# A four-layer graph network on one core: a filler ahead of the first data, quarter work of layer 2 gathered, folding cut, last projections reordered

## The chip, the cores and the metric

The kernel runs on one core of a Trainium2 chip. The time is the device time of one execution in microseconds; the figure for the kernel before is the median of three runs. A profile of one further execution is used to see where the time goes. Engines are called TensorE (PE, with PEld for its weight loads), VectorE (DVE), ScalarE (ACT), GpSimd (POOL) and SyncE (SP), which issues the DMAs.

## What is computed

The input x is 128 graphs of 64 nodes with 512 features (float32), with one 64 by 64 adjacency matrix `adj`. Four layers follow, each of the form `x = x + f(relu(layernorm(x)))`:

```python
# layer 0: 8 heads of 64, masked softmax attention
q, k, v = h @ Wq + bq, h @ Wk + bk, h @ Wv + bv
x = x + softmax(q k^T / 8 + mask) v
# layer 1: the same, with an output projection:  x = x + (attention) @ Wo + bo
# layer 2: no softmax
rel = adj.T * ((h Wq^T) (h Wk^T)^T)
x = x + (rel / norm(rel, axis=2)) (h Wv^T)
# layer 3: attention without biases, o = (attention) @ w_proj + b_proj
x = x + o + layernorm(o) * gamma + beta
```

All of it is float32.

## The kernel before

**Tiling.** Eight graphs, 512 tokens, make a block. There are `NB` = 16 blocks per layer and N = 64 block steps, walked by one loop, `for n in range(N)` (line 976), layer by layer. A block's tokens lie in four tiles of 128 tokens (`NT`); features in four chunks of 128 (`KC`). The state between layers goes through DRAM.

**Projections.** A 512 by 512 by 512 projection is done by Strassen's scheme (Winograd's form, `projection`, line 535): seven products of 256-sided blocks, each four 128x256 matmuls (eight records in a trace). `sums_x` forms the four sums of the input's blocks, `sums_w` (350) those of the weight's blocks (WT1 to WT4). The products run in the order `ORDER = (1, 6, 5, 2, 7, 3, 4)`; they use three PSUM banks in turn (`ps_mm`, tile "mm"), which VectorE and ScalarE evict. Products 1 and 2 read only the input blocks of tokens 0 to 255.

**Quarter work.** Two graphs share a tile of 128 tokens, so scores, weighted sums and relations of one graph are 64 wide and run on 64-row parts of TensorE, four at a time (`QUARTERS`). They write the two "so" buffers (`ps_so`). `attend` (651) does the scores, softmax and the turn of the weights, and calls `finish0` or `finish13` for the weighted sum. `relate` (870) is layer 2: it multiplies hT by gT (gT holds h times the folded matrix Wq^T Wk), masks (`rel`), squares (`sq`), sums the squares by matmuls with a column of ones, and weighs v. There the quarter matmuls stand in three groups: the relation; the sums with the first half of the weighing; the second half.

**Folding.** While layer 0 runs, `fold` (397) multiplies wq2 and wk2 into a2d, transposes wv2 on TensorE into v2d, and multiplies the bias bv1 of layer 1's v through wo1 into a row b1.

**Start.** The first block of x, then q0's weight blocks are loaded (`load_w`, 336: W11, b12, W22, W21). Layer norm of block 0 writes transposes through `ps_t`, which has one buffer, and ScalarE copies them into hT. VectorE sums q0's and k0's weights.

**End.** The output projection of a block follows in the next step, after that step's v: step 63 runs q, k, v of block 63 and then o of block 62. The last block's own output projection is a plain one, tile by tile, with its layer norm per tile (lines 1045 to 1069).

**Order.** Operations are recorded by `Plan` and put in order by a list scheduler (`Plan.order`, 130) with estimated durations; within an engine a step that reads an "mm" tile is preferred by `RUSH` places. The order of recording comes from generators that are spawned with a delay counted in products (`spawn`, `tick`, 934 to 945). The order on every engine is then fixed in the program. Line 192, through which every operation is issued, is the line that a trace shows for nearly all.

Of the kernel before, what the change touches and what calls it, by code (L numbers as in the profile page):

```python
# [12 lines left out]
F32 = mybir.dt.float32  # L13
U16 = mybir.dt.uint16
AF = mybir.ActivationFunctionType
ALU = mybir.AluOpType
# [27 lines left out]
ORDER = (1, 6, 5, 2, 7, 3, 4)  # L44

# [173 lines left out]
RUSH = 60  # L219
AHEAD = 16  # L220
# [37 lines left out]
def gnn_stack_kernel(  # L258
# [37 lines left out]

    def dma(dst, src):
        plan.sync.dma_start(dst, src)
# [6 lines left out]
    def row_bc(name, src):  # L305
        t = rows.tile([P, D], F32, tag="row", name=name)
        dma(t, src.partition_broadcast(P))
        return t
# [27 lines left out]
    def load_w(name, src):  # L336

        w = wp.tile([P, 7, 2, H2], F32, tag="w", name=name)
        b12 = p2.tile([P, 2, H2], F32, tag="b12", name=f"b12_{name}")

        def part(i, j):
            return src[i * H2 : (i + 1) * H2, j * H2 : (j + 1) * H2].rearrange("(c p) f -> p c f", p=P)

        dma(w[:, W11], part(0, 0))
        dma(b12, part(0, 1))
        dma(w[:, W22], part(1, 1))
        dma(w[:, W21], part(1, 0))
        return w, b12
# [43 lines left out]
    def raw(tag, src, nm):  # L392
        t = p1.tile([P, KC, D], F32, tag=tag, name=nm)
        dma(t, src.rearrange("(c p) f -> p c f", p=P))
        return t

    def fold():

        rq, rk = raw("oT", wq2, "rq"), raw("SO", wk2, "rk")
        yield 8  # L400
        for dc in range(KC):
            pa = ps_t.tile([P, D], F32, tag="t", name=f"pfa_{dc}")
            plan.begin()
            for ec in range(KC):
                pe.matmul(pa, rq[:, ec, ts(dc, P)], rk[:, ec, :], start=(ec == 0), stop=(ec == KC - 1))
            plan.end()
            f = p2.tile([P, D], F32, tag="z", name=f"fa_{dc}")
            act.copy(f, pa)
            yield 1
            dma(a2d[dc * P : (dc + 1) * P, :], f)  # L410
            yield 1
        rv, ro = raw("oT", wv2, "rv"), raw("SO", wo1, "ro")
        yield 8
        for dc in range(KC):
            pt = ps_t.tile([P, D], F32, tag="t", name=f"pft_{dc}")
            plan.begin()
            for ec in range(KC):
                pe.transpose(pt[:, ts(ec, P)], rv[:, ec, ts(dc, P)], ident)
            plan.end()
            f = p2.tile([P, D], F32, tag="z", name=f"ft_{dc}")  # L420
            act.copy(f, pt)
            yield 1
            dma(v2d[dc * P : (dc + 1) * P, :], f)
            yield 1

        bvm = p2.tile([P, KC, P], F32, tag="z", name="bvm")
        dve.tensor_copy(bvm, bvc1.unsqueeze(2).to_broadcast([P, KC, P]))
        pb = ps_t.tile([P, D], F32, tag="t", name="pb")
        plan.begin()
        for ec in range(KC):  # L430
            pe.matmul(pb, bvm[:, ec, :], ro[:, ec, :], start=(ec == 0), stop=(ec == KC - 1))
        plan.end()
        b1 = row_bc("b1", bo1)
        dve.tensor_tensor(b1, pb, b1, ALU.add)
        R["b1"] = b1
# [17 lines left out]
    hTs, Ss = {}, {}  # L453
# [13 lines left out]
    def layer_norm(n):  # L467
# [19 lines left out]
        if n == 0:  # L487
            for t in range(NT):
                z = xins[n][t]
                act.activation(z, z, AF.Relu, bias=nb[:, t : t + 1], scale=rs[:, t : t + 1])  # L490
                pt = ps_t.tile([P, KC, P], F32, tag="t", name=f"pz_{n}_{t}")
                plan.begin()
                for c in range(KC):
                    pe.transpose(pt[:, c, :], z[:, ts(c, P)], ident)
                plan.end()
                act.copy(hT[:, :, ts(t, P)], pt)
# [38 lines left out]
    def projection(prod, w, xop, nm, emit):  # L535
# [13 lines left out]
        for i in ORDER:  # L549
# [23 lines left out]
            if i != ORDER[-1]:  # L573
                yield
# [194 lines left out]
    def finish13(n):  # L769
        def done(aTs, v):  # L770
# [19 lines left out]
            for g, po in enumerate(pos):  # L790
                for b in range(2):
                    act.copy(o5[:, b, 2 * g : 2 * g + 2], po[:, b])
# [77 lines left out]
    def relate(n, hT, gT, v):  # L870

        prt = ps_so.tile([P, 2, D], F32, tag="so", name=f"pr_{n}")
        pr = prt[:, 0, : NT * G].rearrange("p (t i) -> p t i", t=NT)
        plan.begin()
        for p in range(NT):
            for kc in range(KC):
                for b in range(2):
                    at = ts(2 * p + b, G)
                    pe.matmul(
                        pr[half(b), p, :], hT[:, kc, at], gT[:, kc, at], start=(kc == 0), stop=(kc == KC - 1)  # L880
                    )
        plan.end(300)
        yield 1
        rel = p2.tile([P, NT, G], F32, tag="s", name=f"rel_{n}")
        dve.tensor_tensor(rel, pr, adj2.unsqueeze(1).to_broadcast([P, NT, G]), ALU.mult)
        yield 1
        sq = p2.tile([P, NT, G], F32, tag="aT", name=f"sq_{n}")
        act.activation(sq, rel, AF.Square)
        yield 6
        assert ("xo", n) in ready and ("v", n) in ready  # L890

        pqs = prt[:, 1, :NT], prt[:, 0, NT * G : NT * G + NT]
        pos = [ps_so.tile([P, 2, 2, H2], F32, tag="so", name=f"pv_{n}_0")]

        def weigh(g, po):
            for p in range(2):
                for b, y in QUARTERS:
                    j = b ^ y
                    pe.matmul(
                        po[half(y), j, p, :], rel[half(b), 2 * g + p, :],  # L900
                        v[half(b), 2 * g + p, j * H2 : (j + 1) * H2], start=True, stop=True,
                    )

        plan.begin()
        for p in range(NT):
            for b, y in QUARTERS:
                pe.matmul(
                    pqs[b ^ y][half(y), p : p + 1], sq[half(b), p, :], ones[half(b), :], start=True, stop=True
                )
        weigh(0, pos[0])  # L910
        plan.end(300)
        ss = sm.tile([P, 2, NT], F32, tag="ss", name=f"ss_{n}")
        for j in range(2):
            dve.tensor_copy(ss[:, j], pqs[j])
        pos.append(ps_so.tile([P, 2, 2, H2], F32, tag="so", name=f"pv_{n}_1"))
        plan.begin()
        weigh(1, pos[1])
        plan.end()
        rn = sm.tile([P, 2, NT], F32, tag="rn", name=f"rn_{n}")
        gps.tensor_tensor(rn.rearrange("p j t -> p (j t)"), ss.rearrange("p j t -> p (j t)"), mhalf, ALU.pow)  # L920
        yield 1
        for t in range(NT):
            for j in range(2):
                xo = xos[n][:, t, j * H2 : (j + 1) * H2]
                dve.scalar_tensor_tensor(xo, pos[t // 2][:, j, t % 2], rn[:, j, t : t + 1], xo, ALU.mult, ALU.add)
            yield t % 2
        store(n, xos[n])
# [31 lines left out]
    for name, got in zip(("q0", "k0"), first):  # L959
        W[name] = got[0]  # L960
        now(sums_w(*got, dve))
# [13 lines left out]
    pending_out = None  # L975
    for n in range(N):
# [3 lines left out]
        if n == 3 * NB // 16:  # L980
            spawn(fold(), 2)
        if l == 0 and k == 9 * NB // 16:
            want("q1")
        if l == 2 and k == NB // 2:
            R["bp"], R["gam"], R["bet"] = row_bc("bp", bp3), row_bc("gam", gam3), row_bc("bet", bet3)
        if n + 1 < N:
            load_x(n + 1)
            spawn(layer_norm(n + 1), 5 if l != 2 else 2)
        if l != 2:
            qT = p1.tile([P, KC, T], F32, tag="qT", name=f"qT_{n}")  # L990
            q_emit = emit_bias(region_T(qT), (bqc0, bqc1)[l]) if l < 2 else emit_plain(region_T(qT))
            run(projection(prod_T, W[f"q{l}"], xop, f"q_{n}", q_emit))
# [11 lines left out]
            spawn(attend(n, qT, kT, v, done), 3)  # L1004
# [4 lines left out]
        else:  # L1009
# [4 lines left out]
            v = p1.tile([P, NT, D], F32, tag="v", name=f"v_{n}")  # L1014
            spawn(relate(n, hTs[n], gT, v), 2)
            spawn(load_xo(n), 2)
# [4 lines left out]

        if pending_out is not None:
            m = pending_out
            lm = m // NB
            assert ("xo", m) in ready and m in SOs
            sop = lambda m=m: SOs[m]
            if lm == 1:
                run(projection(prod_N, W["o1"], sop, f"o_{m}", emit_out1(m)))
                spawn(tail1(m))
                if m == 2 * NB - 1:  # L1030
                    want("k3")
            else:
                o = p1.tile([P, NT, D], F32, tag="kT", name=f"o_{m}")
                run(projection(prod_N, W["o3"], sop, f"o_{m}", emit_out3(m, o)))
                spawn(tail3(m, o))
        pending_out = n if l in (1, 3) else None
        if l in (1, 3):
            spawn(load_xo(n), 4)
# [7 lines left out]
    o3 = p1.tile([P, NT, D], F32, tag="kT", name="o_last")  # L1046
    mv = sm.tile([P, NT, 2], F32, tag="mv", name="mv_last")
    rs = sm.tile([P, NT], F32, tag="rs", name="rs_last")
    for t in range(NT):
# [15 lines left out]
        gps.tensor_tensor(xo, xo, o, ALU.add)  # L1065
# [39 lines left out]
```

## Time and profile before

| | us |
|---|---|
| median of three runs | 2864.86 (2864.85 to 2867.84) |
| the profiled execution's own time | 2866.66 |
| its span, first to last instruction | 2864.9 |
| busy: PE, PEld | 2839.8, 2459.5 |
| busy: DVE, ACT, POOL | 1990.4, 1281.1, 1833.9 |
| granted TensorE clock, mean | 0.999 |

Busy shares are means over stages with different limits. In the lines of the chain of work that ended last, the columns are start, length and what ran, with the number of records. In lines of the timeline they are start, length, engine, source line, operation, output and inputs by the names of the program's buffers, shapes and count, and in brackets the idle time before and what ended it. A ring's buffers share a name: "mm" and "so" are the PSUM tiles named above, "t" is `ps_t`, "kT" also holds the output of a projection in layer 3, "s" also rel, "aT" also sq, "qT" also gT, "oT" and "SO" also raw weights during folding. The end of a matmul is modelled; the spacing of records is more exact than their length.

### The profile page before, as it was taken

How to read it: one execution, taken by the hardware profiler on the slowest of the kernel's cores; microseconds unless marked ns; L12 is line 12 of the kernel's file. 1: busy time of each engine (PE TensorE's matmuls, PEld its weight loads, DVE VectorE, ACT ScalarE, POOL GpSimd, SP SyncE). 2: the span in 40 equal slices, each digit the busy share in tenths (PEclk: the TensorE clock that was granted, in tenths of full speed). 3: DMA queues.
4: the chain of work that ended last, by engine and by line, in shares of the span. 5: the costliest groups of instructions: out<-in, count | busy, mean ns of one | idle time of the engine just before them, and what ended most of it. 6: DMA issues, size and time to landing. Idle time of an engine off the chain costs nothing.

```text
span 2864.9 us, 62358 instructions
## 1 busy us (share of the span) xinstructions
PE 2839.8 (99%) x26080; PEld 2459.5 (86%) x26080; DVE 1990.4 (69%) x3019; ACT 1281.1 (45%) x1656; POOL 1833.9 (64%) x1349
## 2 busy tenths in 40 slices
PE   8999999999999999999999999999999999999998
PEld 7888888888888888888888888888888888888887
DVE  6767777877757657567566554555588788888787
ACT  4554555454554534534534434344334444444441
POOL 5556566656766657657677343435578688787796
PEclk9999999999999999999999999999999999999999
DMA  5675656566443533534546656565433433533531
GB/s 148 164 170 128 141 132 144 121 131 165 104 119 79 124 95 85 134 78 96 130 115 170 149 139 157 142 142 147 103 85 95 116 83 90 126 85 86 129 71 63
DMA packets 629515, 342.31 MB, mean 119 GB/s; under 512 B 480880, under 2 KB 559984, under 8 KB 629232
## 3 DMA queue, kind: packets, MB, share of 16 engines
q1 hardware_dynamic: 629232, 338.32, 48.9%
q8 instruction: 204, 3.34, 0.5%
q14 instruction: 79, 0.65, 0.1%
HBM read 153.66 MB, written 69.21 MB: 78 GB/s over the span
## 4 chain that ended last, share of the span: by engine, by line
PE 97%; DVE 2%; issue 1%; POOL 1%; DMA 0%; ACT 0%; POOLq 0%; DVEq 0%; ACTq 0%
PE mm L192 87%; PE so L192 9%; PE t L192 1%; DVE z L192 0%; DVE st L192 0%; DVE kT L192 0%; POOL s L192 0%; DVE xo L192 0%; DVE zp L192 0%; POOL S L192 0%; DVE u L192 0%; DVE mv L192 0%; DMA xin<-in_x_dram 0%; DVE sr L192 0%; POOL ve L192 0%
## 5 line engine op out<-in xcount | busy, mean ns | idle before, releaser
L192 PE MATMUL mm<-S,w 128*128 128x256 f32 x3584 | 819.8, 380 | 3.8 <-DVE kT L192 1.3
L192 PEld LDWEIGHTS mm<-S,w 128*128 128x128 f32 x3584 | 676.8, 190 | 104.0 <-issue 8.4
L192 PE MATMUL mm<-hT,w 128*128 128x256 f32 x2688 | 632.7, 381 | 0.2 <-ACT s L192 0.2
L192 DVE TENSOR_TENSOR u<-mm,s 128x512 f32<-128x512 f32 x414 | 285.3, 689 | 476.3 <-PE mm L192 336.6
L192 PEld LDWEIGHTS mm<-hT,w 128*128 128x128 f32 x2688 | 509.6, 190 | 75.3 <-issue 5.4
L192 PE MATMUL mm<-w,S 128*128 128x256 f32 x2048 | 472.6, 381 | 0.7 <-DVE kT L192 0.6
L192 PEld LDWEIGHTS mm<-w,S 128*128 128x128 f32 x2048 | 385.3, 190 | 55.8 <-DVE kT L192 1.5
L192 PE MATMUL mm<-w,hT 128*128 128x256 f32 x1536 | 366.3, 381 | 0.0
L192 ACT COPY hT<-hp 128x1024 uint16<-128x1024 uint16 x252 | 334.1, 1359 | 71.4 <-DMA hp<-zp 55.5
L192 ACT COPY s<-mm 128x512 f32<-128x512 f32 x207 | 121.0, 585 | 532.2 <-PE mm L192 438.0
L192 POOL TENSOR_TENSOR s<-s,mx 128x1024 f32<-128x1024 f32 x96 | 184.2, 1920 | 251.7 <-DVE mx L192 251.7
L192 PEld LDWEIGHTS mm<-w,hT 128*128 128x128 f32 x1536 | 289.1, 190 | 41.0 <-issue 0.5
L192 ACT COPY aT<-hp 128x1024 uint16<-128x1024 uint16 x188 | 253.3, 1352 | 155.4 <-DMA hp<-zp 155.2
L192 POOL TENSOR_TENSOR xo<-xo,row 128x512 f32<-128x512 f32 x192 | 283.1, 1494 | 4.3 <-DMA xo<-x 3.3
L192 DVE COPY zp<-s 128x1024 uint16<-128x1024 uint16 x188 | 276.5, 1494 | 2.8 <-POOL s L192 2.0
L192 DVE COPY zp<-xin 128x1024 uint16<-128x1024 uint16 x252 | 241.9, 973 | 39.0 <-ACT xin L192 33.1
L192 ACT ACTIVATE xin<-xin,nb,rs 128x512 f32<-128x512 f32 x256 | 196.0, 812 | 104.9 <-DVE nb L192 104.9
L192 PE MATMUL mm<-w,SO 128*128 128x256 f32 x992 | 224.3, 379 | 0.0
L192 POOL TENSOR_TENSOR S<-hT 128x512 f32<-128x512 f32 x126 | 162.1, 1287 | 94.6 <-ACT hT L192 94.6
L192 PEld LDWEIGHTS mm<-w,SO 128*128 128x128 f32 x992 | 188.4, 190 | 26.0 <-issue 0.4
L192 POOL TENSOR_TENSOR s<-s,sr 128x1024 f32<-128x1024 f32 x96 | 187.4, 1963 | 27.4 <-DVE sr L192 26.5
L192 POOL TENSOR_TENSOR v<-u,z 128x512 f32<-128x512 f32 x64 | 82.2, 1285 | 183.6 <-DVE u L192 169.5
(100 smaller groups left out, 3600.3 us busy)
## 6 DMA issues: line engine op xcount, KB each, us to landing
xin<-x SPq DMA_DIRECT2D x192, 256.0 KB, 3.9
xo<-x SPq DMA_DIRECT2D x64, 512.0 KB, 5.6
xin<-in_x_dram SPq DMA_DIRECT2D x64, 256.0 KB, 3.2
x<-xo SPq DMA_DIRECT2D x64, 256.0 KB, 2.5
x<-xo SPq DMA_DIRECT2D x128, 128.0 KB, 2.5
x<-xo SPq DMA_DIRECT2D x32, 512.0 KB, 3.0
out_dram<-xo SPq DMA_DIRECT2D x30, 512.0 KB, 2.8
xo<-in_x_dram SPq DMA_DIRECT2D x32, 256.0 KB, 3.7
```

Of the source, the lines that this page charges most:

```text
L192: getattr(getattr(self.nc, eng), op)(*a, **k)
```

## The change

- 22 transposes of the identity into a "t" tile are put ahead of everything on TensorE.
- The first projection (q of block 0) has the order (1, 2, 5, 6, 3, 7, 4). Every weight loads W21 second. q0's weight sums go to GpSimd. The first transposes use the three "mm" banks; ScalarE copies the first, VectorE the other three.
- `fold` no longer multiplies bv1 through wo1: layer 1's weighted sum gets the bias at eviction, on VectorE in place of ScalarE's copy. wv2 is transposed by a u16 copy, a transposing DMA and a copy back (`turn`).
- `relate` takes up the block before: one group holds that block's norm sums and weighing and this block's relation. Each norm sum is made once instead of twice; two copies cross the halves. A last call in layer 3 finishes layer 2's last block. The relation uses the "t" tile.
- In the last step the output projection of block 62 comes before v of block 63, and the last block's attention starts without delay. The last tiles' residual addition goes from GpSimd to VectorE. Two output tiles use a weight buffer.

```diff
+ORDER0 = (1, 2, 5, 6, 3, 7, 4)
+WARM = 22
+    pw = ps_t.tile([P, KC, P], F32, tag="t", name="pw")
+    for i in range(WARM):
+        pe.transpose(pw[:, i % KC, :], ident, ident)
         dma(w[:, W11], part(0, 0))
+        dma(w[:, W21], part(1, 0))
         dma(b12, part(0, 1))
         dma(w[:, W22], part(1, 1))
-        dma(w[:, W21], part(1, 0))
...
-        for dc in range(KC):
-            pt = ps_t.tile([P, D], F32, tag="t", name=f"pft_{dc}")
-            for ec in range(KC):
-                pe.transpose(pt[:, ts(ec, P)], rv[:, ec, ts(dc, P)], ident)
-            f = p2.tile([P, D], F32, tag="z", name=f"ft_{dc}")
-            act.copy(f, pt)
+        for ec in range(KC):
+            f = p2.tile([P, KC, P], F32, tag="z", name=f"ft_{ec}")
+            turn(f, rv[:, ec, :], f"v2_{ec}")
             yield 1
-            dma(v2d[dc * P : (dc + 1) * P, :], f)
+            dma(v2d.rearrange("(c p) e -> p c e", p=P)[:, :, ts(ec, P)], f)
-        for ec in range(KC):
-            pe.matmul(pb, bvm[:, ec, :], ro[:, ec, :], start=(ec == 0), stop=(ec == KC - 1))
-        dve.tensor_tensor(b1, pb, b1, ALU.add)
...
-                pt = ps_t.tile([P, KC, P], F32, tag="t", name=f"pz_{n}_{t}")
+                pt = ps_mm.tile([P, KC, P], F32, tag="mm", name=f"pz_{n}_{t}")
-                act.copy(hT[:, :, ts(t, P)], pt)
+                (dve.tensor_copy if t else act.copy)(hT[:, :, ts(t, P)], pt)
...
-                    act.copy(o5[:, b, 2 * g : 2 * g + 2], po[:, b])
+                    at = o5[:, b, 2 * g : 2 * g + 2]
+                    if n // NB == 1:
+                        bias = bvc1.unsqueeze(1).unsqueeze(3).to_broadcast([P, 2, KC, G])
+                        dve.tensor_tensor(at, po[:, b], bias, ALU.add)
+                    else:
+                        act.copy(at, po[:, b])
...
+    held = []
+    def relate(n, hT=None, gT=None):
+        prt = ps_t.tile([P, D], F32, tag="t", name=f"pr_{n}")
+        old = held.pop() if held else None
+        plan.begin()
+        if old:
+            m, rel, sq, v = old
+            for p in range(NT):
+                for b in range(2):
+                    pe.matmul(pq[half(b), p : p + 1], sq[half(b), p, :], ones[half(b), :], start=True, stop=True)
+            for g in range(2):
+                po = ps_so.tile([P, 2, 2, H2], F32, tag="so", name=f"pv_{m}_{g}")
+                for p in range(2):
+                    for b, y in QUARTERS:
+                        pe.matmul(po[half(y), j, p, :], rel[half(b), 2 * g + p, :], ...)
+        if hT is not None:
+            for p in range(NT):
+                for kc in range(KC):
+                    for b in range(2):
+                        pe.matmul(pr[half(b), p, :], hT[:, kc, at], gT[:, kc, at], ...)
+        plan.end(300)
+        if old:
+            dve.tensor_copy(ss[:, 0], pq)
+            for b in range(2):
+                dve.tensor_copy(ss[half(b), 1], pq[half(1 - b)])
+            gps.tensor_tensor(rn, ss, mhalf, ALU.pow)
+        if hT is not None:
+            dve.tensor_tensor(rel, pr, adj2.unsqueeze(1).to_broadcast([P, NT, G]), ALU.mult)
+            act.activation(sq, rel, AF.Square)
+        yield 1
+        if old:
+            for t in range(NT):
+                for j in range(2):
+                    dve.scalar_tensor_tensor(xo, pos[t // 2][:, j, t % 2], rn[:, j, t : t + 1], xo, ALU.mult, ALU.add)
+            store(m, xos[m])
...
-        now(sums_w(*got, dve))
+        now(sums_w(*got, gps if name == "q0" else dve))
+        if n == 3 * NB:
+            spawn(relate(n), 5)
-            spawn(attend(n, qT, kT, v, done), 3)
+            spawn(attend(n, qT, kT, v, done), 3 if n < N - 1 else 0)
+            if n == N - 1:
+                project(n)
             run(projection(prod_N, W[f"v{l}"], xop, f"v_{n}", emit_plain(region_N(v))))
...
-            spawn(relate(n, hTs[n], gT, v), 2)
-            spawn(load_xo(n), 2)
+            spawn(relate(n, hTs[n], gT), 2)
+            spawn(load_xo(n), 6)
...
-    o3 = p1.tile([P, NT, D], F32, tag="kT", name="o_last")
+    o3 = wp.tile([P, NT, D], F32, tag="w", name="o_last")
-        gps.tensor_tensor(xo, xo, o, ALU.add)
+        dve.tensor_tensor(xo, xo, o, ALU.add)
```

`project(n)` holds the output projection of the block before, which stood at the end of the loop's body.

## The prediction

> **What bounds the kernel now.** I read the busy shares first.
>
> ```profile
> PE 2839.8 (99%) x26080; PEld 2459.5 (86%) x26080; DVE 1990.4 (69%) x3019; ACT 1281.1 (45%) x1656; POOL 1833.9 (64%) x1349
> PE 97%; DVE 2%; issue 1%; POOL 1%; DMA 0%; ACT 0%; POOLq 0%; DVEq 0%; ACTq 0%
> ```
>
> TensorE is busy for all but 25.1 us, and the chain that ended last (second line) runs over it. Of the 25.1 us, 11.9 follow the last product and some 8 lie before 15.1 us; the waits of TensorE show 4.7 us in the stage of layer 3 and next to nothing in layers 0 to 2. So only three things count: TensorE work removed, TensorE's late start, and what follows its last product. To price TensorE work I read the chain in order of time over one block of layer 2 (start, length, what):
>
> ```profile
> 1605.10 14.01 PE mm L192 x64
> 1619.11 1.49 PE so L192 x48
> 1620.60 1.92 PE mm L192 x8
> 1622.53 1.02 PE so L192 x16
> 1623.55 8.83 PE mm L192 x40
> 1632.38 2.02 PE so L192 x64
> ```
>
> The six pieces make 29.29 us, one block. "mm" are Strassen products (8 records each), "so" the work on 64-row quarters. Elsewhere in that chain 152 mm records take 33.00 and 64 take 14.01: 0.2158 each, so 1.73 us a product, plus 0.20 once per run. Every return from quarter work costs that 0.20.
>
> **Layer 2: three entries per block become one.** By rate (spacing of records in the timeline), the 64 records of hT by gT take 64 x 0.029 = 1.84; the 32 of the norm sums, 0.49 together (0.0153 each); a weighing of 16 records, 16 x 0.0456 = 0.73. Against the pieces 2.02, 1.49 and 1.02 each entry itself costs 0.18 to 0.28. The changed block has mm in one run, 14.01 + 48 x 0.2158 = 24.37, and one quarter group: 16 sum records (four pairs fewer per block: each sum once, the other half reached by a copy on VectorE) 0.25 + 32 weighings 1.46 + entry and hT by gT 2.02 = 3.73. Sum 28.10, a gain of 1.19.
>
> [...] The row: both groups of a block that are joined differ in form, 64*64 for sums and weighings, 128*64 for hT by gT, and the trace nowhere has the two next to each other. [...] Then a switch inside the group costs again about what an entry costs here, 0.18 to 0.28. [...] I take 1.0, nearest to the entries measured. Fifteen blocks 15 us; the first block lacks the old sums, and the last old group goes as an extra one into layer 3: together another 1. **16 us**, between 12 (a switch costs twice an entry) and 18.6.
>
> What lies beside: VectorE does 8 accumulations (0.41 each) in one burst after the group instead of two of four, and waits ahead of them for the power on POOL (rn 1.65 us, possibly behind a 1.27 us sum). Behind it in its queue are the evictions of product banks. From the group's middle that is 0.8 + 2.5 + 3.3 = 6.6 us; TensorE ends product 7, the next that VectorE must evict, some 6 to 7 us after the same point, and its bank is asked for two products (3.4 us) later. So nothing is late. The loads of xo move by four products, 6.9 us; their six issues (3.8 us on SP) then stand beside those of xin. The statistics of xin wait behind them, but begin 8 us after the present issue has ended.
>
> **Fold.**
>
> ```profile
> 196.61 0.60 PE L192 MATMUL t<-ident,oT 128*128 128x128 f32 x4
> 197.04 1.89 PE L192 MATMUL mm<-S,w 128*128 128x256 f32 x8
> 217.85 3.60 PE L192 MATMUL t<-SO,z 128*128 128x512 f32 x8
> 221.29 3.62 PE L192 MATMUL mm<-w,S 128*128 128x256 f32 x16
> ```
>
> A quartet of transposes holds TensorE for 0.43, four of them 1.7; the bias product 3.44. Both leave: **5.2 us**, all on the bound engine. In exchange VectorE makes four u16 copies (0.65 to 1.5), ScalarE four of 1.35 instead of 0.59, SP issues four more transposing DMAs (about 1.3 each); in layer 0 VectorE is 76% busy without TensorE waiting once, so I cost them at nothing; uncovered they are at most 4 x 1.5 = 6. In layer 1 VectorE takes the oT evictions from ScalarE, to add the bias: 4 x 0.69 per block of 52.8, on an engine 63% busy there. In one block the evictions follow their group at once (1471.83), their sums end at 1479, and the product that reads them comes over 20 us later: nothing.
>
> **Start.** The timeline of TensorE (start, length, idle before):
>
> ```profile
> 6.50 1.11 PE L192 MATMUL t<-ident,xin 128*128 128x128 f32 x4 [6.50 <-ACT xin L192]
> 8.29 1.12 PE L192 MATMUL t<-ident,xin 128*128 128x128 f32 x4 [0.68 <-ACT hT L192]
> 10.99 3.42 PE L192 MATMUL mm<-hT,w 128*128 128x256 f32 x8
> 14.25 0.60 PE L192 MATMUL t<-ident,xin 128*128 128x128 f32 x4
> 15.09 1.99 PE L192 MATMUL mm<-hT,w 128*128 128x256 f32 x8 [0.24 <-ACT s L192]
> ```
>
> The first product takes 3.42 where later ones take 1.73, transposes 1.11 where later ones take 0.60: half speed until about 14.2, though the granted clock reads 1.00. From 15.09 there is no gap; two products of q are done at 16.82. In the change the identity is ready at 1.3; 22 transposes at the slow spacing of 0.24 end by 6.7. If they lift the speed, then: transposes of tokens 0 and 1 at 6.5 and 7.35 (three banks now, no wait for the copy; ScalarE's two normalisations end at 7.3), the second copy on VectorE 8.0 to 8.65, product 1 to 10.4, transposes of tokens 2 and 3 to 11.1, product 2 (now second; it needs only tokens 0 and 1 and block W21, loaded second) to 12.8. S0 is written by 12.75 after two more copies. Weight sums move to POOL: b12, now third (present landing in that place about 9.1), gives the first sum at 10.4, the second at 11.7, wanted at 12.8 and 14.5. (Later weights load in the same new order, but blocks ahead of their use.) So two products are done at 12.8 instead of 16.82: **4.0 us**.
>
> [...] The row: full speed came 3.2 us after the first product, but 7.7 after the first transposes, which ran with gaps; it fits either cause. [...] By it product 1 starts near 9.7 at half speed, ends at 13.1, product 2 near 15.7: a gain of 1.1. I take 4.0, because the new filler is gapless for 5 us, which the old transposes were not, and a gap of 1.32 us at 2306 left the next products at full rate; 1.1 is kept for the range.
>
> **End.**
>
> ```profile
> 2851.98 1.03 PE L192 MATMUL mm<-w,oT 128*128 128x256 f32 x4
> 2855.20 0.68 DVE L192 TENSOR_TENSOR kT<-mm,row 128x512 f32<-128x512 f32 x1
> 2859.34 0.78 POOL L192 TENSOR_SCALAR ve<-mv 128x1 f32<-128x1 f32 x1 [0.48 <-DVE mv L192]
> 2861.16 0.75 DVE L192 SCALAR_TENSOR_TENSOR xo<-z,rs,xo 128x512 f32<-128x512 f32 x1 [0.46 <-POOL rs L192]
> ```
>
> The last product ends at 2853.0, but its eviction starts at 2855.2: VectorE is behind, with block 62's tail in its queue until 2850. The change puts block 62's projection ahead of the last v, so that tail is done some 12 us earlier. A last tile then costs VectorE 3.3 against 3.45 on TensorE (16 x 0.2158), and it is not late. After the last product, in the new order: eviction 0.7, two passes of tile 2 1.3, statistics 0.85, the two POOL steps 1.4 to 1.7 (xo's addition, moved to VectorE, lies beside them), last pass 0.75, store 3.0: 8.2 instead of 11.9. With 0.4 for the gap at 2835, which v products now fill, **4.1 us**, between 2 and 5.5.
>
> **Sum.** 16 + 5.2 + 4.0 + 4.1 = 29.3, taken from the span 2864.9: 2835.6. The profiled execution took 2866.66, 1.8 more than its span; the median of the runs is 2864.86, practically the span, so I take the gain from that: 2835.6.
>
> **Rivals.**
> 1. *The filler does not lift the speed.* For it: [...]the 3.2 us above. Gain 26.4: 2838.5.
> 2. *VectorE becomes the bound of layer 2.* If rn comes a further 3.4 + 1 us late, each block stalls 1 us, 16 in all: 2851.6; with half of it 2843. For it: in-order queue with eight accumulations in one burst. Against: VectorE is 52% busy in layer 2.
> 3. *Slower.* Layer 1's bias additions: should VectorE wait at them, with product evictions queued behind, for a quarter group, it takes more than 2.2 us per block (29.3 + 5.7 = 35 over 16 blocks) to end above 2870.6; with 3 us, 2883.6. Against: VectorE idles 19 us per block there, and the evictions need 2.8.
> 4. *No effect in layer 2*[...]: gain 13 to 17, 2849.
>
> **How the numbers follow.** Likeliest 0.50; rival 1 0.27; rival 2 0.12, mostly in its half form; rival 4 0.05; rival 3 0.03; 0.03 for a gain beyond 36, should layer 3's 4.7 us of waits vanish too. Range: upward the cold start, half of rival 2 and 2 from the end reach 2844; downward 18.6 in layer 2 and layer 3's waits reach 2829. A measurement tells 0.2% (5.7 us) from no change. Faster 0.95, same 0.02, slower 0.03.
>
> **What would show it.** Layer 2's block near 28.3 us with one run of mm; the first product at 8.7 taking 1.8 (not 3.4); no mm gap before 680; the last eviction within 0.2 of the last product's end, the span's end about 8 after. Wrong if TensorE shows waits on VectorE in layer 1 or 2.

## The result, and the profile after

The median after is 2849.68 us (four runs, 2848.25 to 2851.76), before 2865.99 us in the same set (four runs, 2864.85 to 2867.84). The ratio is 0.9943 with an interval of 0.9926 to 0.9960: the kernel became 16.3 us faster, where 29.3 were forecast; two later sets gave 15.6 and 15.4. The time lies outside the predicted range (2829 to 2844); the direction was right. The profiled execution of after took 2849.34 us, its span is 2847.6 (before 2866.66 and 2864.9), so the two traces have 17.3 us to share out. In lines of the changed kernel the recording line is L193, not L192.

The busy shares and the chain that ended last:

```profile
PE 2829.3 (99%) x25822; PEld 2469.7 (87%) x25822; DVE 2039.3 (72%) x3104; ACT 1246.9 (44%) x1589; POOL 1847.4 (65%) x1349
PE 96%; DVE 2%; POOL 1%; issue 1%; DMA 0%; ACT 0%; POOLq 0%; DVEq 0%
```

TensorE is still the bound, busy for all but 18.3 us (25.1 before). To see where the 17.3 us come from I number the 11,656 records of the Strassen products (128x256) in both traces and subtract the start of the k-th after from that before. Both kernels do them in nearly the same order, so a difference that grows or shrinks between two of them places a gain or a loss:

| stretch | predicted | measured | gained so far |
|---|---|---|---|
| two products of q done (15.1 against 16.9) | 4.0 | 1.85 | 1.85 |
| 15 to 117 us, in steps at 37 to 64 us | 0 | -0.60 | 1.25 |
| fold, 117 to 246 us | 5.2 | 5.20 | 6.45 |
| 246 to 461 us, most of it at 443 | 0 | -0.96 | 5.49 |
| 461 to 1523 us (layer 1 lies within) | 0 | 0.00 | 5.49 |
| layer 2, with its extra group in layer 3 | 16 | 8.92 | 14.41 |
| layer 3, at 2690 us | 0 | -0.36 | 14.05 |
| gap before the last v, now filled | 0.4 | 0.58 | 14.63 |
| from the last product's end to the end | 3.7 | 2.67 | 17.30 |

Layer 2 is missing 7.1 of the 12.0 us, the start with what it gives back 2.75, two places where other engines' queues are late 1.3, the tail 1.0. One block of layer 2, in the chain in order of time (start, length, what):

```profile
1594.11 0.50 PE t L193 x14
1594.61 0.05 PE so L193
1594.67 0.01 PE t L193
1594.67 1.78 PE so L193 x30
1596.45 2.02 PE t L193 x64
1598.47 24.37 PE mm L193 x112
1622.84 0.50 PE t L193 x14
```

From 1594.11 to 1622.84 is a block: 28.73 us against 29.29. The products form one run of 24.37, as forecast to the hundredth. The quarter group takes 4.36 instead of 3.73 (3.92 with the cost of a form change that the forecast allowed for). The start, from the timeline of TensorE:

```profile
1.34 4.69 PE L193 MATMUL t<-ident 128*128 128x128 f32 x22 [1.34 <-POOL ident masks.py:199]
6.43 0.66 PE L193 MATMUL mm<-ident,xin 128*128 128x128 f32 x4 [0.39 <-ACT xin L193]
7.30 0.66 PE L193 MATMUL mm<-ident,xin 128*128 128x128 f32 x4 [0.21 <-ACT xin L193]
8.78 3.51 PE L193 MATMUL mm<-hT,w 128*128 128x256 f32 x8 [0.83 <-ACT xin L193]
12.09 1.22 PE L193 MATMUL mm<-ident,xin 128*128 128x128 f32 x8
13.14 1.89 PE L193 MATMUL mm<-hT,w 128*128 128x256 f32 x8
15.07 2.18 PE L193 MATMUL mm<-S,w 128*128 128x256 f32 x9
```

The transposes behind the filler take 0.66 (1.11 before): the filler does lift the speed. Yet the first product, which starts at 8.78 as forecast, takes 3.51. The table of windows shows the granted clock (the third number from the right) in that stretch:

```profile
8.70:9.70 1.00, 0.92 (x3) 0.80 (x4) 0.05 (x1) 0.81 (x1) 1.00 (x1) 0.67 1.26 186
9.70:10.70 1.00, 1.00 (x4) 0.81 (x3) 0.00 (x0) 0.00 (x0) 0.92 (x2) 0.50 1.07 333
11.70:12.70 1.00, 1.00 (x6) 0.80 (x5) 0.00 (x0) 0.37 (x1) 1.00 (x2) 0.63 1.07 197
```

The clock had been full since 5.62 us; it was at half from 9.03 to 12.44 us. The tail, TensorE, VectorE and GpSimd in turn:

```profile
2837.35 1.03 PE L193 MATMUL mm<-w,oT 128*128 128x256 f32 x4
2838.78 0.68 DVE L193 TENSOR_TENSOR w<-mm,row 128x512 f32<-128x512 f32 x1
2840.23 0.75 DVE L193 SCALAR_TENSOR_TENSOR xo<-z,rs,xo 128x512 f32<-128x512 f32 x1
2840.90 0.69 DVE L193 BATCH_NORM_STATS2 st<-w 128x6 f32<-128x512 f32 x1
2841.89 0.57 POOL L193 TENSOR_SCALAR ve<-mv 128x1 f32<-128x1 f32 x1 [2.29 <-DVE mv L193]
2843.50 0.75 DVE L193 SCALAR_TENSOR_TENSOR xo<-z,rs,xo 128x512 f32<-128x512 f32 x1 [0.46 <-POOL rs L193]
```

The last eviction follows the last product's end (2837.35 + 1.03) after 0.40, where it stood 2.2 late before. One VectorE pass of block 62's tail in the kernel before bears on that lateness:

```profile
2835.49 5.14 DVE L192 SCALAR_TENSOR_TENSOR z<-kT,mv,row 128x512 f32<-128x512 f32 x1
```

The same operation takes 0.7 to 1.8 us in the rest of the kernel's tail.

### The profile page after: what moved, and what is told of

Its sections match the earlier page's. It is cut to its first block, busy times and chain, and to the rows that moved or that the text cites. A ratio compares the mean times of both kernels' runs of the same rounds, so it can differ in the third digit from the quotient of the medians.

```text
span 2847.6 us, 61907 instructions
## 1 busy us (share of the span) xinstructions
PE 2829.3 (99%) x25822; PEld 2469.7 (87%) x25822; DVE 2039.3 (72%) x3104; ACT 1246.9 (44%) x1589; POOL 1847.4 (65%) x1349
## 3 DMA queue, kind: packets, MB, share of 16 engines
q8 instruction: 202, 3.31, 0.5%
## 4 chain that ended last, share of the span: by engine, by line
PE 96%; DVE 2%; POOL 1%; issue 1%; DMA 0%; ACT 0%; POOLq 0%; DVEq 0%
PE mm L193 86%; PE so L193 8%; PE t L193 2%; DVE z L193 1%; DVE zp L193 0%; DVE st L193 0%; DVE xo L193 0%; POOL s L193 0%; DVE kT L193 0%; DMA hp<-zp 0%; DVE u L193 0%; POOL S L193 0%; DVE sr L193 0%; DMA xin<-in_x_dram 0%; DVE w L193 0%
## 5 line engine op out<-in xcount | busy, mean ns | idle before, releaser
L193 PE MATMUL mm<-S,w 128*128 128x256 f32 x3584 | 817.3, 380 | 3.7 <-DVE kT L193 1.3
L193 PEld LDWEIGHTS mm<-S,w 128*128 128x128 f32 x3584 | 678.2, 190 | 98.7 <-issue 2.6
L193 PE MATMUL mm<-hT,w 128*128 128x256 f32 x2688 | 631.8, 380 | 1.2 <-ACT xin L193 0.8
L193 DVE TENSOR_TENSOR u<-mm,s 128x512 f32<-128x512 f32 x414 | 285.2, 689 | 459.3 <-PE mm L193 303.8
L193 PEld LDWEIGHTS mm<-hT,w 128*128 128x128 f32 x2688 | 510.3, 190 | 72.1 <-ACT xin L193 1.0
L193 PE MATMUL mm<-w,S 128*128 128x256 f32 x2048 | 472.8, 381 | 1.9 <-DVE kT L193 1.4
L193 PEld LDWEIGHTS mm<-w,S 128*128 128x128 f32 x2048 | 385.2, 190 | 56.5 <-DVE kT L193 2.2
L193 ACT COPY hT<-hp 128x1024 uint16<-128x1024 uint16 x252 | 333.6, 1348 | 77.7 <-DMA hp<-zp 77.5
L193 PE MATMUL mm<-w,hT 128*128 128x256 f32 x1536 | 366.0, 381 | 0.0
L193 ACT COPY s<-mm 128x512 f32<-128x512 f32 x207 | 120.6, 583 | 523.8 <-PE mm L193 444.4
L193 POOL TENSOR_TENSOR s<-s,mx 128x1024 f32<-128x1024 f32 x96 | 184.4, 1922 | 239.6 <-DVE mx L193 239.5
L193 PEld LDWEIGHTS mm<-w,hT 128*128 128x128 f32 x1536 | 289.3, 190 | 41.2 <-ACT v L193 0.8
L193 ACT COPY aT<-hp 128x1024 uint16<-128x1024 uint16 x188 | 253.1, 1352 | 158.9 <-DMA hp<-zp 158.6
L193 POOL TENSOR_TENSOR xo<-xo,row 128x512 f32<-128x512 f32 x192 | 286.8, 1512 | 4.3 <-DMA xo<-x 4.3
L193 DVE COPY zp<-s 128x1024 uint16<-128x1024 uint16 x188 | 275.5, 1488 | 4.0 <-POOL s L193 3.8
L193 DVE COPY zp<-xin 128x1024 uint16<-128x1024 uint16 x252 | 242.7, 979 | 40.0 <-ACT xin L193 34.5
L193 ACT ACTIVATE xin<-xin,nb,rs 128x512 f32<-128x512 f32 x256 | 196.0, 808 | 97.5 <-DVE nb L193 93.6
L193 PE MATMUL mm<-w,SO 128*128 128x256 f32 x992 | 224.5, 379 | 0.0
L193 POOL TENSOR_TENSOR qT<-u,z 128x512 f32<-128x512 f32 x64 | 89.7, 1402 | 190.4 <-DVE u L193 172.7
L193 PEld LDWEIGHTS mm<-w,SO 128*128 128x128 f32 x992 | 188.4, 190 | 25.6
L193 POOL TENSOR_TENSOR s<-s,sr 128x1024 f32<-128x1024 f32 x96 | 187.5, 1965 | 24.3 <-DVE sr L193 23.3
L193 POOL TENSOR_TENSOR S<-hT 128x512 f32<-128x512 f32 x126 | 162.1, 1286 | 42.2 <-ACT hT L193 42.1
```

The costliest lines, as they stand in the source:

```text
L193: getattr(getattr(self.nc, eng), op)(*a, **k)
```

## Experiments

Ten runs were made, two of them of the changed kernel again. A single profiled execution of each is read with the same comparison of product starts; medians are given where several executions were timed. Throughout, a time is its span plus 1.8 us.

**1. Each norm sum once, in the kernel before.** The forecast priced the 32 sum records at 0.49 together, and half as many at 0.25.

```diff
         for p in range(NT):
-            for b, y in QUARTERS:
-                pe.matmul(pqs[b ^ y][half(y), p : p + 1], sq[half(b), p, :], ones[half(b), :], start=True, stop=True)
+            for b in range(2):
+                pe.matmul(pqs[1][half(b), p : p + 1], sq[half(b), p, :], ones[half(b), :], start=True, stop=True)
...
-        for j in range(2):
-            dve.tensor_copy(ss[:, j], pqs[j])
+        dve.tensor_copy(ss[:, 0], pqs[1])
+        for b in range(2):
+            dve.tensor_copy(ss[half(b), 1], pqs[1][half(1 - b)])
```

> The kernel before, where layer 2 alone makes each norm sum once (16 records per block in two quarters) instead of twice (32 records in all four), with the crossing copies of the change; its three groups per block stay. Theory of the prediction (cost by number of records): each block loses 16 x 0.0153 = 0.25 us, 29.29 to 29.05, 3.9 us in all. Rival (cost by the number of records per quarter, which the edit leaves as it was, since the two quarters that are left do all the work): the block stays at 29.29 within 0.05, and the 16 records are spaced 0.03 instead of 0.015.

The time was 2867.27 us (span 2865.5). In the chain of the run, the group of sums and first weighing:

```profile
1605.57 14.01 PE mm L192 x64
1619.58 1.48 PE so L192 x30
1621.06 1.92 PE mm L192 x8
...
1632.84 2.02 PE so L192 x64
1634.86 14.01 PE mm L192 x64
```

The block stays at 29.29 (1605.57 to 1634.86). The group has 16 sums where there were 32 and takes 1.48 instead of 1.49. In the timeline of TensorE, first of the kernel before, then of this one, the sums take as long in both: the weighings begin 0.49 after the first sum, save for two records in this run that begin 0.1 sooner:

```profile
1619.04 0.64 PE L192 MATMUL so<-ones,aT 64*64 64x1 f32 x32
1619.53 1.07 PE L192 MATMUL so<-v,s 64*64 64x256 f32 x16
```

```profile
1619.51 0.57 PE L192 MATMUL so<-ones,aT 64*64 64x1 f32 x14
1619.90 0.43 PE L192 MATMUL so<-v,s 64*64 64x256 f32 x2
1619.94 0.20 PE L192 MATMUL so<-ones,aT 64*64 64x1 f32 x2
1620.00 1.06 PE L192 MATMUL so<-v,s 64*64 64x256 f32 x14
```

Sixteen records on two quarters take what 32 on four took: 8 steps of 0.061 in either case. What is paid is the step, not the record. Making each sum once gained nothing in the block. Most of the 0.6 by which this span is above that of the kernel before (0.5) lies at the start, where its clock rose at 16.05 us and not at 14.08.

**2. A second change of form in the joined group, in the changed kernel.** The relation is put between the sums and the weighing, so that the group changes its form twice, 64\*64 to 128\*64 and back.

```diff
                     pe.matmul(pq[half(b), p : p + 1], sq[half(b), p, :], ones[half(b), :], start=True, stop=True)
+        if hT is not None:
+            for p in range(NT):
+                for kc in range(KC):
+                    for b in range(2):
...
+                        pe.matmul(pr[half(b), p, :], hT[:, kc, at], gT[:, kc, at], start=(kc == 0), stop=(kc == KC - 1))
+        if old:
             pos = []
...
-        if hT is not None:
-            for p in range(NT):
...
```

> The changed kernel with hT by gT (128*64 form) moved between the norm sums and the weighing (64*64 form), so that the joined group changes its form twice instead of once; nothing else differs. [...] the block of layer 2 grows from 28.73 by 0.08 (what an entry costs on the quarter side by the result: 0.28 less the 0.20 of the run of products) to 0.28. If it costs nothing: 28.73 within 0.03.

The time was 2850.03 us (span 2848.2). Its chain:

```profile
1593.36 2.58 PE t L193 x80
1595.94 1.89 PE so L193 x32
1597.83 24.37 PE mm L193 x112
...
1626.66 24.37 PE mm L193 x112
```

The block is 28.83 against 28.73: the further change costs 0.10. So a change of form does cost something here, but about half of the least that the forecast allowed (0.18 to 0.28, estimated from the entries), and it doesn't explain the missing 0.44 to 0.63 a block. The row that explains more is the second: 32 weighings standing alone take 1.89, where 16 standing alone took 1.02 in the kernel before. The 16 more take 0.87, 0.054 each, where the forecast had 0.0456.

**3. No filler.**

```diff
-WARM = 22
+WARM = 0
```

> The changed kernel without the 22 transposes ahead of the first data. Theory now (transposes lift TensorE's speed, but it falls again before the first product, which then runs slowly with or without the filler): the four transposes of tokens 0 and 1 take 1.1 each instead of 0.66, the first product starts some 0.5 to 0.9 later and still takes about 3.5, the whole is 0 to 1 us longer than the changed kernel. Rival 1 of the prediction (transposes never lift the speed): transposes of tokens 0 and 1 take the same with and without filler, no difference in time. The step as predicted (filler saves 2.9 us): 2.9 us longer.

The median was 2850.90 us (2850.01 to 2852.27), the ratio to the kernel before 0.9948 (0.9934 to 0.9963). The timeline of its TensorE:

```profile
6.46 1.12 PE L193 MATMUL mm<-ident,xin 128*128 128x128 f32 x4 [6.46 <-ACT xin L193]
8.23 1.12 PE L193 MATMUL mm<-ident,xin 128*128 128x128 f32 x4 [0.65 <-ACT xin L193]
10.17 3.75 PE L193 MATMUL mm<-hT,w 128*128 128x256 f32 x8 [0.83 <-ACT xin L193]
```

The transposes are slow again and the first product starts 1.4 later. The two products are done 0.6 later than in the kernel before, not 1.1 earlier as the cold rival had it; the clock rose at 16.1 in this execution and at 14.1 in that one. By the profiles TensorE ends 3.0 us later than in the changed kernel; by the medians it is 1.2 (0.9 to 1.3 with the later repeats of the changed kernel), less than the executions of one kernel differ. So the runs don't settle what the filler is worth in time.

**4. The gaps in the transposes filled too.** In the changed kernel TensorE was busy for 58% of the 3.41 us ahead of the fall of the clock. If the clock fell for want of work, which was a guess, work in the gaps should hold it.

```diff
-WARM = 22
+WARM = 25
+MORE = (2, 4, 0, 0)
...
                     pe.transpose(pt[:, c, :], z[:, ts(c, P)], ident)
+                for i in range(MORE[t]):
+                    pe.transpose(pw[:, i % KC, :], ident, ident)
```

> The changed kernel with 25 transposes of the identity ahead, two more after the transposes of token tile 0 and four after those of tile 1, so that TensorE has hardly a gap before the first product. Theory now (the speed fell at 9.0 us because TensorE was busy for only half of the 3.4 us before): the first product takes 1.9 instead of 3.5, two products are done near 13.3 instead of 15.0, and the end comes up to 1.7 us earlier, less what the wait on ScalarE's copies near 45 us takes back. Rival (the speed is given by something else than the gaps, such as a fixed time after the start): the first product still takes 3.5, and the time is that of the changed kernel or 0.3 more.

The median was 2849.51 us (2847.85 to 2850.00), the span 2846.0. From its timeline:

```profile
6.93 0.38 PE L193 MATMUL t<-ident 128*128 128x128 f32 x2
7.30 0.65 PE L193 MATMUL mm<-ident,xin 128*128 128x128 f32 x4
7.79 0.60 PE L193 MATMUL t<-ident 128*128 128x128 f32 x4
8.48 0.66 PE L193 MATMUL mm<-ident,xin 128*128 128x128 f32 x4
8.98 1.89 PE L193 MATMUL mm<-hT,w 128*128 128x256 f32 x8
...
11.54 1.99 PE L193 MATMUL mm<-hT,w 128*128 128x256 f32 x8 [0.24 <-ACT s L193]
```

The first product takes 1.89 and the two products are done at 13.37, a gain of 3.54: within 0.5 of the 4.0 forecast. But this profile is of the fastest of the four executions, and so are the other two profiles with this filling (experiments 6 and 7) of theirs; the median is only 0.2 below that of the changed kernel, which is no difference that these runs can tell.

**5. The old order of the last step.**

```diff
-            spawn(attend(n, qT, kT, v, done), 3 if n < N - 1 else 0)
-            if n == N - 1:
-                project(n)
+            spawn(attend(n, qT, kT, v, done), 3)
```

> The changed kernel with only the order of the last step put back: block 63's v before block 62's output projection, and its attention after the old delay. The addition on VectorE and the output tiles stay. Theory (the order gives the 2.7 us after the last product, because VectorE then has block 62's tail behind it): VectorE is late again, the last eviction starts 2 us or more after the last product's end, that stretch grows from 9.2 to 11 to 12, and the gap ahead of the last quarter group (0.6 us) is back: 2.5 to 3.4 us longer. Rival (moving the addition from GpSimd to VectorE gives it, or takes it): the stretch stays within 0.5 of 9.2.

The time was 2850.16 us (span 2848.4). A gap of 0.64 between two starts is back at 2820 us, and from the end of the last product (2837.03 + 1.03 in the timeline) 10.33 us pass, 1.15 more than with the new order: neither the 11 to 12 of the theory nor within 0.5 of 9.2. On VectorE the last eviction starts only 0.7 late (2838.76), not 2 or more; tile 2's statistics come behind it (2839.36). So the new order is worth 0.6 before the last product and 1.15 behind it; the other 1.5 of the tail's 2.67 remain with the old order, so they belong to the rest of the change (the addition moved to VectorE and the other buffers of the output touch this stretch; neither was run alone). The traces show one thing more: the pass of 5.14 us is there in both kernels that have the old tail (5.13 in experiment 1), beside four additions on GpSimd; here, with the old order and such additions too, the passes in its place take 1.44 and 1.38. That it made VectorE late is likely; why it was so long was not tested.

**6. The changed kernel again, a rearranged tail, and one eviction moved.** These ask where the small losses sit. In the changed kernel ScalarE evicts block 0's v; its copy stands behind a copy of block 1's hT that waits for a transposing DMA. ScalarE, then TensorE in the timeline of the changed kernel:

```profile
43.73 1.36 ACT L193 COPY hT<-hp 128x1024 uint16<-128x1024 uint16 x1 [1.41 <-DMA hp<-zp]
44.96 0.57 ACT L193 COPY z<-mm 128x512 f32<-128x512 f32 x1
```

```profile
45.59 3.72 PE L193 MATMUL mm<-w,S 128*128 128x256 f32 x16 [0.43 <-ACT z L193]
```

The first of the two edits lets VectorE make the later copy, for block 0 alone. The second, on top of experiment 4, puts each last tile's closing passes behind the next tile's statistics.

```diff
-    def emit_plain(region):
+    def emit_plain(region, z5=act):
...
-                act.copy(b, a)
+                (act.copy if z5 is act else z5.tensor_copy)(b, a)
...
-            run(projection(prod_N, W[f"v{l}"], xop, f"v_{n}", emit_plain(region_N(v))))
+            run(projection(prod_N, W[f"v{l}"], xop, f"v_{n}", emit_plain(region_N(v), act if n else dve)))
```

```diff
+        def finish(t=t, o=o, xo=xo, at=at):
+            dve.tensor_tensor(xo, xo, o, ALU.add)
...
+            dma(target(3, NB - 1)[t], xo)
+        if t:
+            late()
+        late = finish
+    late()
```

> The changed kernel with one eviction elsewhere: z5 of block 0's v goes to VectorE instead of ScalarE, where it stands behind the copies of block 1's hT that wait for their transposing DMAs. Theory (the 0.6 us stall of TensorE at 45 us is that eviction queued behind those copies): no gap over 0.3 us between 40 and 50 us, the gain of the start is kept to 117 us, 0.4 to 0.6 us earlier there for the same clock history. Rival (the stall is a VectorE or bank shortage of the new order): the gap stays, under another name.

> The gaps filled as before, and in the last four tiles the two last passes and the addition of a tile come after the statistics of the next, so that the last tile's statistics wait for nothing but its eviction. Theory: the first product runs at full speed in any execution; the last pass comes 0.5 to 0.7 us sooner after the last product (5.1 to 5.3 instead of 5.9 for the end of it). Together 1 to 2.5 us under the changed kernel run beside it. Rival (VectorE's work after the last product is the same sum in any order): no gain from the tail.

> The changed kernel as it is, once more, as a control for the next one and for how much one start differs from another. Theory now (when the speed goes up or down at the start depends on where a fixed raster of 3.4 us falls, which differs from execution to execution): two products are done at 13.3 or at 15.0 us, or between, with the same program; medians scatter by 2 us. Rival (the start is the same in every execution): two products done at 15.0 again.

The changed kernel again: its two products were done at 15.69, later than the 13.3 to 15.0 expected.

The eviction moved: 2848.61 us in one execution (span 2846.8). No wait of TensorE is left between 40 and 50 us, and of 1.86 us gained at the second product 1.96 stand at 117 us, where the changed kernel has 1.25 of 1.85. The two profiles with the moved eviction (this and experiment 7) gain 0.1 in that stretch; the eight other profiles of the changed kernel and its variants lose 0.2 to 1.1. So the loss, 0.60 in the changed kernel's profile, lies in ScalarE's queue.

The tail rearranged: the median is 2849.02 us (2847.97 to 2849.64), the changed kernel beside it 2849.57 (2849.08 to 2851.60). Its VectorE reads:

```profile
2837.69 0.68 DVE L193 TENSOR_TENSOR w<-mm,row 128x512 f32<-128x512 f32 x1
2838.41 0.69 DVE L193 BATCH_NORM_STATS2 st<-w 128x6 f32<-128x512 f32 x1
...
2842.19 0.75 DVE L193 SCALAR_TENSOR_TENSOR xo<-z,rs,xo 128x512 f32<-128x512 f32 x1
```

From the last product's end at 2837.03 to the last pass's end at 2842.94 are 5.91 us, in the changed kernel 5.87 (2838.38 to 2844.25). The statistics come earlier, but the passes put off follow them on the same engine and the sum is the same: no gain from the tail. The median is 0.55 lower than the changed kernel's, and the ranges overlap by as much, so no gain is shown for the whole either.

**7. Experiment 4's transposes and the moved eviction together,** beside the changed kernel once more.

> Two edits that each gained by the profile are put together: 25 transposes ahead and 6 between the first transposing groups, and the first block's v evicted (z5) by VectorE, not ScalarE. If they add, the two products are done 3.5 us earlier than in the kernel before, no gap above 0.4 stands between 40 and 50 us, TensorE's last product ends some 16.5 us earlier than before (11 in the changed kernel with a half-speed first product, 16.1 with the transposes alone), the span is about 2845.5 and the median 0.5 to 2 us under the changed kernel beside it. Rival: the gain is lost again at one of the later fixed-order waits (443 us, 2690 us), because a TensorE that is earlier only waits longer there: then the product times agree with the changed kernel's after 443 us and the medians too.

> The changed kernel once more, as the measure for the run beside it. Median 2849.5 within 1; the start shows either a first product of 3.5 (the speed had fallen back) or of 1.9 to 2.0, as the beat of the clock falls, and the span follows by up to 2 us.

The two together took 2848.86 us (2848.20 to 2849.06, five runs; ratio to before 0.9943, 0.9929 to 0.9956), the changed kernel 2850.00 (2848.62 to 2851.18, five runs). The median is 1.1 lower; the ranges overlap by 0.4. By the profiles its TensorE ends 1.85 earlier, which agrees in direction. The gain at the second product is 2.81, not the 3.5 expected: the first product started at 9.71, because the second tile of x landed later (VectorE waits 0.68 us for its DMA, which it does not in experiment 4; the tile's transposes begin at 8.03 instead of 7.30). The clock rose at 7.08, not 5.30. Of it 2.95 stand at 117 us, and no gap above 0.4 is left between 40 and 50 us. But the rival expectation has a share: 0.6 is lost at 180 us, as in experiment 4, and the gap at 443 stays, so 6.63 are left there, less than the 6.91 of experiment 4 alone. TensorE ends 15.8 earlier than in the kernel before, where some 16.5 were expected (the changed kernel's own figure is 14.6, not the 11 named there). Of the medians over several executions its is the lowest, 0.16 below the rearranged tail: less than these runs can tell.

## Why the prediction was wrong

**Layer 2 (16 forecast, 8.92 measured): the step that failed.** It read "a weighing of 16 records, 16 x 0.0456 = 0.73" and "16 sum records ... 0.25". Both price single records, but what is paid is the step of starts: in the trace of the kernel before, the four records of a weighing's step start within 0.02 us of each other, and the next four 0.22 later. The 16 more weighings of experiment 2 are four steps and take 0.87, 0.22 a step. From the first start of a weighing to the last are about 0.70, which I divided among the records; the last four's own 0.22 fell outside, and most of it was booked as "entry". Likewise the sums are eight steps in both kernels and take 0.47 (1.49 less 1.02), however many records they have (experiment 1).

Priced so, the joined group holds 0.47 of sums and 1.74 of weighings, 0.50 more than the forecast's 0.25 and 1.46. An entry into quarter work costs 0.20 on the following run of products, which the forecast had right, and 0.15 in the group (1.02 less its four steps), not 0.18 to 0.28. The relation is 2.02 with such an entry, as forecast. These make 4.23; the measured 4.36 leaves 0.13 for the change of form inside the group, near the 0.10 that a second one cost in experiment 2. Two entries fewer per block are worth 0.70, less 0.13 makes 0.57, and 0.56 was measured; 16 times that is 9.0. The change of form is real and small, 0.10 to 0.13; that it costs as much as an entry was an estimate, and the 1.0 against 1.19 that I weighed by it was not where the error lay.

**Fold: right,** 5.20 of 5.2, and nothing on VectorE, ScalarE or SP showed on TensorE between 117 and 246 us.

**Start (4.0 forecast, 1.85 measured).** The step "if they lift the speed" held: the transposes take 0.66 (1.11 before) and the first product starts at 8.78 (forecast 8.65). What failed is the silent assumption that the speed then stays. It fell back at 9.03, 3.4 us after it rose, a stretch in which TensorE was idle for four tenths. With the gaps filled (experiment 4) 3.54 came, and the speed held in all three profiles with that filling; but it also held in three of the six profiles that have the changed kernel's own start, so that the idle gaps decide fits and is not shown.

The 1.85 is also one draw among several. In those six profiles the gain at the second product was 0.99, 1.22 and 1.85 where the speed fell back, and 1.86, 2.50 and 3.25 where it held. Two other things moved it. In three of the six the second tile of x landed later (VectorE waits 0.6 to 1.0 us for it, TensorE stands idle 0.88 to 1.26 us ahead of its transposes), and the first product started at 9.4 to 9.8, not 8.7 to 8.8. And in two of the three where the speed held, the third product waited 1.03 and 1.07 us for its sum S, on which VectorE spent 1.8 us: it was written at 14.3 and 14.9, where the forecast had 12.75.

Then 0.60 was lost again where ScalarE's queue releases a product bank late (shown by the moved eviction): I had costed everything between 15 and 117 us at nothing without asking what an earlier TensorE would meet.

**Elsewhere in the first layers and in layer 3.** "No mm gap before 680" was wrong. VectorE's eviction at 443.15 stands behind two copies of 4.09 us together and TensorE's next product is late (0.8 between two starts); one run of quarter work more, 0.28, stands in the new order between 246 and 356 us. At 2690 us two starts lie 1.18 apart instead of 0.52. These 1.3 us were read off and not traced further.

**Layer 1's bias additions: right,** no loss from 461 to 1523 us.

**End (4.1 forecast, 3.25 measured).** The gap gave 0.58 for 0.4. Behind the last product 9.18 us pass instead of 8.2: the eviction is 0.40 late, the two passes of tile 2 take 1.51 instead of 1.3, the last store and what follows 3.31 instead of 3.0, the statistics 0.1 more. The order of the steps was as forecast, but not the reason: the forecast gave the late eviction to the order of block 62's projection, and with the old order (experiment 5) it is late by only 0.7 of the former 2.2.

**The rivals.** The cold start (2838.5), a filler that leaves the speed as it is, was an estimate that the trace of before allowed and didn't show. It has the wrong mechanism, since the filler lifts the speed (0.66 against 1.11 for four transposes), and nearly the right size: 1.1 at the start (a first product of some 3.4 us, like the 3.42 before), where 1.85 was measured and 1.25 kept. VectorE as bound of layer 2 is refuted: TensorE's only wait on it there, 0.63 at 2261.7 us, stands in the kernel before too (0.62). Slower through the bias additions: refuted. "No effect in layer 2", 2849, comes closest in its number, by luck: layer 2 gave half, and the change of form takes 0.13 of the 0.63 a block that are missing from 1.19; several shortfalls add up to the same time.

**The range.** The terms named for its upper end add up to more than it: the cold start (2.9), half of rival 2 (8) and 2 from the end lead from 2835.6 to 2848.5, not to 2844. The measured 2849.68 lies above that too.

## What to carry to other kernels

Price work on quarters of TensorE by steps of starts (here 0.061 us a step of the sums and 0.22 a step of the weighings), and count the last step's own length: here a record count times a mean spacing made a joined group's work 0.50 too cheap, and read 0.18 to 0.28 for an entry that takes 0.15. Behind a filler ahead of the first data, look at the gaps between the first real instructions too: here the speed it won, at 5.62 us, was lost again at 9.03, 0.25 us into the first product. When TensorE moves earlier, look for the first eviction in a fixed queue that stands behind a copy waiting for a DMA: here 0.60 of a gain of 1.85 ended there.

## What the runs showed of the hardware

In the profile of the changed kernel the granted clock is full at 5.62, half at 9.03 and full again at 12.44, 3.41 us apart; in its repeat in experiment 7 it is half from 9.5 to 12.9. When the first rise comes differs between executions: between 4.36 and 7.10 in nine profiles with a filler, at 14.1, 16.0 and 16.1 in three without. In all twelve TensorE was 88 to 100% busy in the 3.41 us ahead of the rise. In five of them (the kernel before, experiments 1, 2, 3 and the filled kernel of 7) it was 60 to 80% busy in the 3.41 us before that, and no rise came at their end. In the nine the work ahead of the rise was transposes alone; the first four transposes of x then take 0.66 in the changed kernel, against 1.11 in the kernel before.

After the rise, three profiles of the changed kernel with 58, 46 and 44% busy in the following 3.41 us fell back to half; the three experiments with 25 transposes and filled gaps (88 to 92%) did not. But three kernels with the changed kernel's own start (experiments 2, 5 and the moved eviction) did not fall either, at 76, 61 and once 50%. So busy share alone doesn't tell these profiles apart: 50% held where 58% fell. What decides was not shown. The executions of the changed kernel spread over 2.5 to 3.5 us, those with filled gaps over 2.2, 1.7 and 0.9 (experiments 4, 6 and 7); how much of that spread comes from the start was not measured.

Before the first rise the granted clock reads 1.00 although TensorE runs at half speed (the first product takes 3.75 in experiment 3, with a reading of 1.00 throughout, against 1.89 in experiment 4 after the rise): there the length of a known record, and not the clock column, tells the speed.
